# A graph, soft-MoE and MoE model on one core: sort, first linears and first dense stage put in hand-written orders

## The chip, the core and the metric

One core of a Trainium2 chip runs the whole model in one launch. The metric is the device time of a launch in microseconds (us). Five engines work side by side, each through its own queue of instructions: TensorE (PE, whose weight loads the profile lists as PEld), VectorE (DVE), ScalarE (ACT), GpSimd (POOL) and SyncE (SP, which here only issues DMAs). Semaphores order work between engines.

## What is computed

1250 nodes with 768 features, 40,000 edges (src, dst), all in f32. Four residual layers follow one another; the change touches the first two thirds of the first one.

```python
def gatv2(x, src, dst, Ws, bs, Wd, bd, attn):
    H, D = attn.shape
    fs = (x @ Ws + bs).reshape(-1, H, D)
    fd = (x @ Wd + bd).reshape(-1, H, D)
    e = jax.nn.leaky_relu(fs[src] + fd[dst], 0.2)
    logits = jnp.einsum('ehd,hd->eh', e, attn)
    m = jax.ops.segment_max(logits, dst, num_segments=N)
    ex = jnp.exp(logits - m[dst])
    denom = jax.ops.segment_sum(ex, dst, num_segments=N)
    alpha = ex / denom[dst]
    out = jax.ops.segment_sum(alpha[:, :, None] * fs[src], dst, num_segments=N)
    return jax.nn.elu(out)

h = gatv2(x, src, dst, W1s, b1s, W1d, b1d, attn1).reshape(N, DIM)   # 8 heads of 96
h = layer_norm(h + x, ln1_w, ln1_b)
out = gatv2(h, src, dst, Wos, bos, Wod, bod, attno).reshape(N, DIM) # 1 head
return layer_norm(out, lno_w, lno_b)
...
x = x + gnn(layernorm(x));  x = x + soft_moe(layernorm(x))
x = x + gcn(layernorm(x));  x = x + top2_moe(layernorm(x))
```

## The kernel before

Nodes go in 10 blocks of 128 (the last has 98). Softmax over the edges of a node is made dense: for each pair of a block of targets and a block of sources there is a table of logits, 128 x 128 x heads, filled with −3e38 first, into which the edges' logits are scattered. So the kernel has these stages, in order of time of the profiled execution:

- **Sort (0 to 511).** Edges are sorted into the 100 pairs of blocks ("buckets"), 512 places each. `sort_edges` (L202) is a generator. Its first pass makes one-hots of the bucket of each edge on DVE (L250, 63 steps of five columns of 128 edges), which PE adds up (L252); L258 turns the totals into starts. Its second pass goes through the 63 steps again: PE makes running counts (L284, L285), ACT keeps the `carry` to the next step (L287), DVE takes each edge's rank (L290, L292), POOL multiplies the one-hots by node numbers (`valued`, L296), DVE makes for each of five columns a one-hot `to` of the place (L302), and PE permutes with it (L304, two matmuls of 512 columns each, added up in one place in PSUM). At the end the sorted node numbers go to DRAM (`idx_d`) and, by arithmetic on DVE and four transposes, into `where`, the row of each edge in its table.
- **First linears, in the same stretch.** `two_linears` (L789) makes fs and fd per block: transposes of x, then for each of two tables two halves of six matmuls of 384 columns (L801), a copy on ACT (L803), bias and product with `a2` on POOL (L805, L811), a sum per head on DVE (L812), and a store on ACT's queue. After each table the sort goes three steps on. A tile scheduler decides the order on every engine here.
- **Fills.** SP loads edges, x, the weights and biases, then issues 100 fills of 512 KB for the 8-head tables (L1489) and 100 of 64 KB for the 1-head tables (L1493).
- **Branch (511 to 528).** If a bucket overflowed, a general path is taken; otherwise the fast one. All inputs here take the fast one.
- **Edge logits 1 (528 to 1251).** Bucket by bucket, in an order written by hand: rows of fs and fd gathered by one-hot matmuls (L392, f32 split in high and low parts), leaky relu and product on DVE (L404), scattered by POOL (L427). A generator `early` goes one step on per bucket; from bucket 85 on it loads the first dense block's tables.
- **Dense 1 (1286 to 1636).** `Dense.run` (L685). After ACT's queue has issued the loads of fs (L702), ten blocks of targets: maxima over 1250 sources for each of eight heads (`begin`, L717 to L725, DVE); per head ACT's exp over 128 x 1280 (L732), ten PE transposes (L737) whose results DVE multiplies by edge counts ct (`aT`, L738), and the matmuls with fs (L750), one head behind (`waiting`). `end` (L752) divides by the denominators, makes the ELU (an exp on ACT, L768), and calls `normalize` (L836): x + g − 1, statistics by `block_stats` (L144, with a Sqrt on ACT at L151), scale, and weight and bias on POOL. The scheduler decides the order. The logits of a block (`lt`, ten pieces of 512 KB) and counts (`ct`) are loaded on SP's queue (L671 and after), two blocks in the buffers.
- **Linears 2 (to 1810), edges 2 (to 2440), dense 2 (to 2640), soft MoE (to 3200), graph convolution (to 3640), MoE (to 4344).**

`reuse_waits="tile"` pools let a tile wait only for the last users of its own buffer. A DMA signals its end on one of a limited number of semaphores, which later DMAs of other queues use again.

Of the kernel before, what the change touches and what calls it, by code (L numbers as in the profile page):

```python
# [8 lines left out]
F32 = mybir.dt.float32  # L9
# [3 lines left out]
I32 = mybir.dt.int32  # L13
# [37 lines left out]
def model(ctx: ExitStack, tc: tile.TileContext, t: dict, out: bass.AP):  # L51
# [150 lines left out]
    def sort_edges(ap, src_i, dst_i, where, full, bulk):  # L202

        from_b = ap.tile([P, P], BF16, name="from_b")
        nc.vector.tensor_sub(from_b, ones, later)
        minus = ap.tile([1, P], FP16, name="minus")
        nc.vector.memset(minus, -1.0)
        limit = ap.tile([1, 1], F32, name="limit")  # L210
        nc.vector.memset(limit, float(LIMIT))
        ones_b = ap.tile([P, P], BF16, name="ones_b")
        nc.vector.tensor_copy(ones_b, ones)
        bucket = ap.tile([P, NBK], BF16, name="bucket")
        nc.gpsimd.iota(bucket, pattern=[[1, NBK]], base=0, channel_multiplier=0,
                       allow_small_or_imprecise_dtypes=True)
        place = ap.tile([P, CAP], FP16, name="place")
        nc.gpsimd.iota(place, pattern=[[1, CAP]], base=1 - LIMIT, channel_multiplier=0,
                       allow_small_or_imprecise_dtypes=True)


        bk = ap.tile([P, ECOLS], BF16, name="bk")
        in_block = [ap.tile([P, ECOLS], F32, name=f"in_block{i}") for i in range(2)]
        nc.vector.memset(bk, 200.0)
        block = []
        for x, y in zip((src_i, dst_i), in_block):
            nc.vector.memset(y, 0.0)
            hi = ap.tile([P, ECOL + 1], I32, name="hi")
            lo = ap.tile([P, ECOL + 1], I32, name="lo")
            hf = ap.tile([P, ECOL + 1], F32, name="hf", bufs=2)  # L230
            block.append(hf)
            for n, s in ((P, slice(0, ECOL)), (ETAIL, slice(ECOL, ECOL + 1))):
                nc.vector.tensor_scalar(hi[:n, s], x[:n, s], 7, None, op0=ALU.arith_shift_right)
                nc.vector.tensor_scalar(lo[:n, s], x[:n, s], 127, None, op0=ALU.bitwise_and)
                nc.vector.tensor_copy(hf[:n, s], hi[:n, s])
                nc.vector.tensor_copy(y[:n, s], lo[:n, s])
                nc.vector.tensor_scalar_add(y[:n, s], y[:n, s], 1.0)
        for n, s in ((P, slice(0, ECOL)), (ETAIL, slice(ECOL, ECOL + 1))):
            nc.vector.scalar_tensor_tensor(bk[:n, s], block[1][:n, s], float(NB), block[0][:n, s],
                                           op0=ALU.mult, op1=ALU.add)  # L240


        hot = ap.tile([P, 2 * STEPS - 1, LANES, NBK], BF16, name="hot")
        tot_p = bulk.tile([P, 2, 512], F32, name="pair")
        for g in range(STEPS):
            for h in range(2):
                c = (g * 2 + h) * LANES
                if c > ECOL:
                    continue
                nc.vector.tensor_tensor(hot[:, g * 2 + h], bk[:, c:c + LANES, None].to_broadcast([P, LANES, NBK]),  # L250
                                        bucket[:, None, :].to_broadcast([P, LANES, NBK]), ALU.is_equal)
                nc.tensor.matmul(tot_p[:, h, :LANES * NBK], ones_b, hot[:, g * 2 + h].rearrange("p l k -> p (l k)"),  # L252
                                 start=(g == 0), stop=(c + 2 * LANES > ECOL))
        first = ap.tile([1, 2 * LANES + 1, NBK], F32, name="first")
        nc.vector.memset(first[:, 0, :], 0.0)
        for l in range(2 * LANES):
            h, i = divmod(l, LANES)
            nc.vector.tensor_add(first[:, l + 1, :], first[:, l, :], tot_p[0:1, h, i * NBK:(i + 1) * NBK])  # L258
        top = ap.tile([1, 1], F32, name="top")
        over = ap.tile([1, NB, NB], F32, name="over")  # L260
        nc.vector.tensor_scalar_add(over.rearrange("p i j -> p (i j)"), first[:, 2 * LANES, :], float(-CAP))
        nc.vector.tensor_scalar_add(over[:, NB - 1, :], over[:, NB - 1, :], float(P))
        nc.vector.tensor_reduce(top, over.rearrange("p i j -> p (i j)"), AX.X, ALU.max)
        nc.vector.tensor_scalar(full, top, 0.0, None, op0=ALU.is_gt)
        yield

        carry = []
        for h in range(2):  # L270
            x = ap.tile([1, LANES * NBK], FP16, name=f"carry{h}", bufs=2)
            nc.scalar.activation(x, first[:, h * LANES:(h + 1) * LANES, :].rearrange("p l k -> p (l k)"),
                                 AF.Relu, bias=limit, scale=-1.0)
            carry.append(x)
        sorted_p = bulk.tile([P, 2, CAP], F32, name="pair")
        for g in range(STEPS):
            for h in range(2):
                c = (g * 2 + h) * LANES
                if c > ECOL:
                    continue  # L280
                o = hot[:, g * 2 + h]
                flat = o.rearrange("p l k -> p (l k)")
                run = bulk.tile([P, 512], F32, name="run", bufs=2)
                nc.tensor.matmul(run[:, :LANES * NBK], from_b, flat, start=True, stop=False)  # L284
                nc.tensor.matmul(run[:, :LANES * NBK], minus, carry[h], start=False, stop=True)  # L285
                x = ap.tile([1, LANES * NBK], FP16, name=f"carry{h}", bufs=2)
                nc.scalar.activation(x, run[0:1, :LANES * NBK], AF.Relu, scale=-1.0)  # L287
                carry[h] = x
                at = ap.tile([P, LANES, NBK], F32, name="at", bufs=2)
                nc.vector.tensor_tensor(at, run[:, :LANES * NBK].rearrange("p (l k) -> p l k", k=NBK), o, ALU.mult)  # L290
                rank = ap.tile([P, LANES], F32, name="rank", bufs=4)
                nc.vector.tensor_reduce(rank, at, AX.X, ALU.add)  # L292
                valued = []
                for i in range(2):
                    v = ap.tile([P, LANES, NBK], BF16, name=f"valued{i}", bufs=2)
                    nc.gpsimd.tensor_tensor(v, o, in_block[i][:, c:c + LANES, None].to_broadcast([P, LANES, NBK]), ALU.mult)  # L296
                    valued.append(v)
                for l in range(LANES):
                    if c + l > ECOL:
                        continue  # L300
                    to = ap.tile([P, CAP], BF16, name="to", bufs=5)
                    nc.vector.tensor_scalar(to, place, rank[:, l:l + 1], None, op0=ALU.is_equal)  # L302
                    for i in range(2):
                        nc.tensor.matmul(sorted_p[:NBK, i, :], valued[i][:, l, :], to,  # L304
                                         start=(c + l == 0), stop=(c + l == ECOL))
                yield


        nodes = ap.tile([NBK, 2, CAP], F32, name="nodes")
        nodes_b = ap.tile([NBK, 2, CAP], BF16, name="nodes_b")  # L310
        nc.vector.tensor_copy(nodes, sorted_p[:NBK])
        nc.scalar.copy(nodes_b, sorted_p[:NBK])
        nc.sync.dma_start(idx_d[:, :], nodes_b.rearrange("k i c -> k (i c)"))
        row = ap.tile([NBK, CAP], F32, name="row")
        none_at = ap.tile([NBK, CAP], F32, name="none_at")
        nc.gpsimd.iota(none_at, pattern=[[0, CAP // P], [1, P]], base=P * P, channel_multiplier=0,
                       allow_small_or_imprecise_dtypes=True)
        empty = ap.tile([NBK, CAP], F32, name="empty")
        nc.vector.scalar_tensor_tensor(row, nodes[:, 1, :], float(P), nodes[:, 0, :], op0=ALU.mult, op1=ALU.add)
        nc.vector.tensor_scalar_add(row, row, float(-P - 1))  # L320
        nc.vector.tensor_scalar(empty, nodes[:, 0, :], 0.0, None, op0=ALU.is_equal)
        nc.vector.tensor_sub(none_at, none_at, row)
        nc.vector.tensor_mul(none_at, none_at, empty)
        nc.vector.tensor_add(row, row, none_at)
        pt = bank()
        for q in range(CAP // P):
            nc.tensor.transpose(pt[:, q, :NBK], row[:, q * P:(q + 1) * P], ident[:NBK, :NBK])
        nc.vector.tensor_copy(where, pt[:, :, :NBK])
# [1219 lines left out]
```

## Time and profile before

| what | us |
|---|---|
| median of 3 runs (lowest to highest) | 4335.69 (4330.73 to 4339.43) |
| the profiled execution | 4345.71 |
| its span, with a mean granted TensorE clock of 0.923 | 4343.8 |
| busy PE / DVE / ACT / POOL | 3758.5 / 2293.6 / 1156.8 / 1413.5 |
| first one-hot of the count pass (L250) starts | 10.6 |
| last permute (L304) ends | 511.4 |
| first gather matmul (L392) | 527.9 |
| first matmul of the second linears (L801) | 1636.0 |

The span is the profiled program from its first to its last record; times in it are told from its start. Stages overlap little: each needs what the one before wrote to DRAM. The page's second part shows the span in 40 equal slices of 108.6 us, in tenths busy; the first five slices are the sort and first linears, slices 12 to 15 the first dense stage:

```
PE   6888699999958889889999493788969996999998
DVE  8555599999968872277777356430452153000000
ACT  0111166666647661122222111110001121111110
POOL 2444378888851112156666400000001001111111
PEclk7999899999979889999999797898989997999999
DMA  9820122321144441245454531004850015898896
```

### The profile page before, as it was taken

Reading aid. Unit: us, or ns where it says so; the run is one execution under the profiler, and the core shown is the slowest. Engines: PE = TensorE matmul, PEld = TensorE weight load, DVE = VectorE, ACT = ScalarE, POOL = GpSimd, SP = SyncE. Lnnn points to the kernel's source line nnn. Section 1 sums busy time; section 2 is a strip of 40 time slices with the busy share of each in tenths; the row PEclk is TensorE's granted clock in tenths of the full one; section 3 lists DMA queues with packets and bytes.
Section 4 is the critical chain, followed back from the end, with each engine's and each line's share of the span. In section 5 each row is a group of like instructions: output and inputs, shape, how many; then the busy total and the mean of one; then the engine's idle time right before and its main releaser. Section 6 shows DMA issues by size and latency. Waiting matters only on the chain.

```text
span 4343.8 us, 53109 instructions
## 1 busy us (share of the span) xinstructions
PE 3758.5 (87%) x19539; PEld 2911.5 (67%) x19539; DVE 2293.6 (53%) x4014; ACT 1156.8 (27%) x3811; POOL 1413.5 (33%) x1273
## 2 busy tenths in 40 slices
PE   6888699999958889889999493788969996999998
PEld 2444399999958775589999462343436785887876
DVE  8555599999968872277777356430452153000000
ACT  0111166666647661122222111110001121111110
POOL 2444378888851112156666400000001001111111
PEclk7999899999979889999999797898989997999999
DMA  9820122321144441245454531004850015898896
GB/s 319 286 75 19 43 71 56 107 57 53 56 129 164 164 140 41 80 61 59 53 50 50 65 101 61 0 6 107 225 97 30 1 41 191 307 328 325 321 333 225
DMA packets 337404, 531.71 MB, mean 122 GB/s; under 512 B 74136, under 2 KB 211632, under 8 KB 337068
## 3 DMA queue, kind: packets, MB, share of 16 engines
q1 hardware_dynamic: 268848, 461.95, 34.9%
q10 hardware_dynamic: 35772, 43.13, 4.6%
q0 software_dynamic: 32512, 23.13, 2.5%
q8 instruction: 155, 2.54, 0.3%
q14 instruction: 117, 0.96, 0.1%
HBM read 426.11 MB, written 105.82 MB: 122 GB/s over the span
## 4 chain that ended last, share of the span: by engine, by line
PE 51%; DMA 8%; DVE 4%; ACT 4%; issue 3%; POOL 1%; ACTq 0%; SPq 0%; POOLq 0%; DVEq 0%
PE z L392 8%; PE bank L1442 8%; PE acc L1452 7%; PE po L750 5%; PE bank L801 4%; PE acc L185 4%; PE acc L953 3%; ACT ex L732 2%; PE acc L1037 2%; PE acc L978 2%; PE acc L1276 2%; DMA lt<-logit 2%; DMA logit<-lg,where 2%; PE bank L1261 2%; DMA x<-fd_d 1%
## 5 line engine op out<-in xcount | busy, mean ns | idle before, releaser
L427 POOL DMA_INDIRECT logit<-lg,where x780 | 803.3, 1030 | 394.5 <-issue 201.5
L404 DVE SCALAR_TENSOR_TENSOR c<-z,a 128x768 f32<-128x768 f32 x680 | 645.2, 951 | 133.8 <-PE z L392 122.9
L392 PE MATMUL z<-sh,oh 128*128 128x388 f32 (+4 forms) x1560 | 550.5, 353 | 75.5 <-ACT lin L411 38.0
L392 PE MATMUL z<-sl,oh 128*128 128x388 f32 (+4 forms) x1560 | 537.1, 344 | 1.0 <-DVE sl L362 1.0
L392 PE MATMUL z<-dl,oh 128*128 128x388 f32 (+5 forms) x1560 | 536.6, 344 | 0.0
L392 PE MATMUL z<-dh,oh 128*128 128x388 f32 (+5 forms) x1560 | 536.3, 344 | 0.0
L392 PEld LDWEIGHTS z<-sh,oh 128*128 128x128 f32 (+1 forms) x1560 | 301.2, 193 | 85.8 <-ACT lin L411 52.0
L1455 DVE TENSOR_SCALAR y<-acc,sl 128x768 f32<-128x768 f32 x27 | 27.5, 1018 | 591.0 <-PE acc L1452 591.0
L1442 PEld LDWEIGHTS bank<-xT,w 128*128 128x128 f32 x2916 | 330.1, 193 | 10.3 <-issue 8.2
L1442 PE MATMUL bank<-xT,w 128*128 128x128 f32 x2916 | 333.0, 276 | 0.4 <-DVE xT L83 0.4
L750 PE MATMUL po<-fs,aT 128*128 128x97 f32 (+4 forms) x2000 | 320.7, 318 | 3.2 <-POOL fs L697 3.2
L1452 PE MATMUL acc<-w,hT 128*128 128x384 f32 x972 | 321.9, 486 | 0.0
L392 PEld LDWEIGHTS z<-sl,oh 128*128 128x128 f32 (+1 forms) x1560 | 301.1, 193 | 1.7 <-DVE sl L362 1.6
L392 PEld LDWEIGHTS z<-dl,oh 128*128 128x128 f32 (+1 forms) x1560 | 299.8, 192 | 0.0
L392 PEld LDWEIGHTS z<-dh,oh 128*128 128x128 f32 (+1 forms) x1560 | 299.4, 192 | 0.1
L750 PEld LDWEIGHTS po<-fs,aT 128*128 128x128 f32 (+1 forms) x2000 | 259.5, 192 | 56.3 <-issue 7.3
L414 DVE TENSOR_REDUCE lg<-c 128x8 f32<-128x768 f32 x290 | 275.6, 950 | 6.5
L1452 PEld LDWEIGHTS acc<-w,hT 128*128 128x128 f32 x972 | 180.7, 190 | 115.3
L737 PE MATMUL bank<-ident,ex 128*128 128x128 f32 (+1 forms) x900 | 131.7, 301 | 143.3 <-ACT ex L732 139.5
L732 ACT ACTIVATE ex<-lt,top 128x1280 f32<-128x1280 f32 (+1 forms) x90 | 222.5, 2516 | 88.1 <-PE bank L737 65.2
L373 DVE TENSOR_SCALAR oh<-idx,own 128x1024 fp32r<-128x1024 bf16 x200 | 230.2, 1151 | 0.6 <-DMA idx<-idx_d 0.6
L304 PE MATMUL pair<-to,valued 128*100 128x512 bf16 x626 | 169.1, 419 | 69.8 <-DVE to L302 69.6
(318 smaller groups left out, 5769.3 us busy)
## 6 DMA issues: line engine op xcount, KB each, us to landing
w<-in_L_ffn_w_dram SPq DMA_DIRECT2D x53, 3456.0 KB
logit<-none SPq DMA_DIRECT2D x100, 512.0 KB
idx<-idx_d SPq DMA_DIRECT2D x200, 256.0 KB
lt<-logit SPq DMA_DIRECT2D x90, 512.0 KB
w<-in_L_ffn_w_dram SPq DMA_DIRECT2D x32, 576.0 KB
w<-in_L_ffn_w_dram ACTq DMA_DIRECT2D x32, 576.0 KB
logit<-lg,where POOLq DMA_INDIRECT x780, 4.3
ct<-pairs_d SPq DMA_DIRECT2D x18, 576.0 KB
```

The source lines that it names most:

```text
L185: nc.tensor.matmul(p[:n, h, :HF], xT[:, k, b * P:b * P + n], w[:, k, h * HF:(h + 1) * HF], start=(k == 0), stop=(row is None and k == KD - 1))
L304: nc.tensor.matmul(sorted_p[:NBK, i, :], valued[i][:, l, :], to, start=(c + l == 0), stop=(c + l == ECOL))
L373: nc.vector.tensor_scalar(oh, idx.rearrange("p (a c) -> p a c", a=2), own, None, op0=ALU.is_equal)
L392: nc.tensor.matmul(z[:, h, :widths[h]], self.oh[:n, a, q * P:(q + 1) * P], rows[b, w][part][:n, h * HW:h * HW + widths[h]], start=(a == 0 ...
L404: nc.vector.scalar_tensor_tensor(halves(c), self.z[q][:, :, :HF], 0.0, halves(attn), op0=ALU.max, op1=ALU.mult, **more)
L414: nc.vector.tensor_reduce(self.lg[:, q, :], self.c[q].rearrange("p (h d) -> p h d", h=heads), AX.X, ALU.add)
L427: nc.gpsimd.indirect_dma_start(out=table[self.k][:, :], out_offset=bass.IndirectOffsetOnAxis(ap=where[:, q, self.k:self.k + 1], axis=0), i ...
L732: nc.scalar.activation(ex[:n], lt[:n, :, h], AF.Exp, bias=top[:n, h:h + 1])
L750: nc.tensor.matmul(o, aT[:, s, :n], f[:, s, :], start=(s == 0), stop=(s == NB - 1))
L801: nc.tensor.matmul(p[:n, :HF], xT[:, k, :n], w[:, k, h * HF:(h + 1) * HF], start=(k == 0), stop=(k == KD - 1))
L1442: nc.tensor.matmul(pt[:, c - c0, :], w1[:, k, c * P:(c + 1) * P], xT[:, k, :], start=(k == 0), stop=(k == KD - 1))
L1452: nc.tensor.matmul(p[:, h, :HF], hT[:, c, :], w2[:, c, h * HF:(h + 1) * HF], start=(c == 0), stop=(c == KH - 1))
```

## The change

Three stretches are given a fixed order on PE, DVE, ACT and POOL (`manual_schedule`); SP stays with the scheduler.

1. `sort_edges` becomes a class `Sort` whose steps are methods, and the main function writes their order: all one-hots (with the counts five steps behind) together with 12 of the 40 half linears; then `totals` and the rank of step 0; then per step the rank of the next step, 28 half linears spread evenly, and the permute of this step. `to` has 15 buffers instead of 5, `valued` 3 instead of 2, y and c of the linears 3 instead of 2. Loads are issued as src, dst, x0, ws, x1, wd, biases, a2, x2 to x9, and then the fills. Layer statistics are taken block by block, two blocks ahead, instead of for all blocks at the start. In `two_linears` the sum per head and the store come two and three half steps later, and the next block's transposes at the end of the block before.
2. Sorted nodes are copied by ACT into two bf16 tiles and stored; the arithmetic of `where` moves into `rows_in_tables`, called in the fast branch before the first edge logits, with the nodes read back from DRAM by ACT's queue.
3. The first dense stage (heads 8) takes its maxima in a generator of 12 steps and a bit, three of them at each of heads 3 to 7 of the block before; those of block 0 run in the last buckets of the edge stage, two steps per bucket. The end of a block is cut in steps, one per head of the next block. Transposes 8 and 9 of a head come first, and go through an ACT copy and a POOL product instead of DVE. x + g moves to POOL, and its −1 is dropped, since the normalization that follows removes a constant. The order for one head (dense 2) stays.

The core of the diff (the bodies of `one_hot`, `count`, `totals` and the constructor hold the old instructions):

```diff
+        def rank(self, n):
+            _, h, c = self.steps[n]
+            ap, o = self.ap, self.hot[:, n]
+            run = self.bulk.tile([P, 512], F32, name="run", bufs=2)
+            nc.tensor.matmul(run[:, :LANES * NBK], self.from_b, self.flat(n), start=True, stop=False)
+            nc.tensor.matmul(run[:, :LANES * NBK], self.minus, self.carry[h], start=False, stop=True)
+            self.carry[h] = ap.tile([1, LANES * NBK], FP16, name=f"carry{h}", bufs=2)
+            nc.scalar.activation(self.carry[h], run[0:1, :LANES * NBK], AF.Relu, scale=-1.0)
...
+            for i in range(2):
+                v = ap.tile([P, LANES, NBK], BF16, name=f"valued{i}", bufs=3)
...
+                    x = ap.tile([P, CAP], BF16, name="to", bufs=3 * LANES)
+                    nc.vector.tensor_scalar(x, self.place, rank[:, l:l + 1], None, op0=ALU.is_equal)
...
+        def store(self):
+            for i in range(2):
+                nodes = self.ap.tile([P, CAP], BF16, name="to", bufs=3 * LANES)
+                nc.scalar.copy(nodes[:NBK, :], self.sorted_p[:NBK, i, :])
+                nc.sync.dma_start(idx_d[:, i * CAP:(i + 1) * CAP], nodes[:NBK, :])
+
+    def rows_in_tables():
...
+            nc.scalar.dma_start(nodes.rearrange("k i c -> k (i c)"), idx_d[:, :])
...
+            nc.vector.scalar_tensor_tensor(row, nodes[:, 1, :], float(P), nodes[:, 0, :], op0=ALU.mult, op1=ALU.add)
...
+                nc.tensor.transpose(pt[:, q, :NBK], row[:, q * P:(q + 1) * P], ident[:NBK, :NBK])
+            nc.vector.tensor_copy(where, pt[:, :, :NBK])
...
+        def maxima(self, b):
+            n, lt = ROWS[b], self.loaded[b][0]
+            self.tops[b] = top = self.even.tile([P, HEADS], F32, name="top", bufs=2)
+            m = self.even.tile([P, P, self.heads], F32, name="m")
+            nc.vector.tensor_tensor(m[:n], lt[:n, :P, :], lt[:n, P:2 * P, :], ALU.max)
+            yield
+            for j in range(2, NB):
+                nc.vector.tensor_tensor(m[:n], m[:n], lt[:n, j * P:(j + 1) * P, :], ALU.max)
+                yield
+            left = P
+            while left > 32:
+                left //= 2
+                nc.vector.tensor_tensor(m[:n, :left, :], m[:n, :left, :], m[:n, left:2 * left, :], ALU.max)
+                yield
+            nc.vector.tensor_reduce(top[:n], m[:n, :left, :].rearrange("p s h -> p h s"), AX.X, ALU.max)
+            nc.vector.tensor_scalar_mul(top[:n], top[:n], -1.0)
+            yield
+
         def early(self, at):
-            for _ in range(at):
+            for k in range(at):
                 yield
-            yield from self.load(0, self.even)
+            for _ in self.load(0, self.even):
+                k += 1
+                yield
+            if self.heads > 1:
+                while k < NBK - 5:
+                    k += 1
+                    yield
+                for n, _ in enumerate(self.maxima(0)):
+                    if n % 2:
+                        yield
...
+                def end_in_steps(b, po):
...
+                    nc.vector.tensor_scalar_min(neg[:n], g[:n], 0.0)
+                    yield
+                    nc.scalar.activation(neg[:n], neg[:n], AF.Exp)
+                    yield
+                    nc.vector.scalar_tensor_tensor(g[:n], g[:n], 0.0, neg[:n], op0=ALU.max, op1=ALU.add)
+                    yield from finish(dp, b, g)
...
+                        ex = dp.tile([P, NB * P], F32, name="ex", bufs=2)
+                        nc.scalar.activation(ex[:n], lt[:n, :, h], AF.Exp, bias=top[:n, h:h + 1])
+                        aT = dp.tile([P, NB, P], F32, name="aT", bufs=2)
+                        for s0, s1 in ((8, NB), (0, 4), (4, 8)):
+                            pt = pp.tile([P, 4, P], F32, name="bank", bufs=4)
+                            for s in range(s0, s1):
+                                nc.tensor.transpose(pt[:, s - s0, :n], ex[:n, s * P:(s + 1) * P], ident[:n, :n])
+                            if s0 == 8:
+                                raw = dp.tile([P, 2, P], F32, name="raw", bufs=2)
+                                nc.scalar.copy(raw[:, :, :n], pt[:, :2, :n])
+                                nc.gpsimd.tensor_mul(aT[:, s0:s1, :n], raw[:, :, :n], ct[:, s0:s1, :n])
+                            else:
+                                nc.vector.tensor_tensor(aT[:, s0:s1, :n], pt[:, :s1 - s0, :n], ct[:, s0:s1, :n], ALU.mult)
+                        if waiting:
+                            product(*waiting)
+                            if waiting[1] == heads - 1:
+                                ending = end_in_steps(waiting[0], waiting[3])
+                        next(ending, None)
+                        if h >= 3:
+                            for _ in range(3):
+                                next(coming, None)
+                        waiting = (b, h, aT, po)
...
                 x = hb[:n, b, :]
-                nc.vector.scalar_tensor_tensor(x, g[:n], -1.0, x, op0=ALU.add, op1=ALU.add)
+                nc.gpsimd.tensor_add(x, x, g[:n])
+                yield
                 mv = dp.tile([P, 2], F32, name="mv", bufs=2)
+                yield
                 block_stats(mv, x, n)
+                yield
                 nc.vector.tensor_scalar(x, x, mv[:n, 0:1], mv[:n, 1:], op0=ALU.subtract, op1=ALU.mult)
...
+        with tc.manual_schedule(engines={mybir.EngineType.PE, mybir.EngineType.DVE,
+                                         mybir.EngineType.Activation, mybir.EngineType.Pool}):
+            normalize(0)
+            normalize(1)
+            nc.vector.tensor_scalar_mul(a2, a2, 0.2)
+            linears = two_linears(linear_tile, hb, normalize, (ws, wd), biases, a2, HEADS, (fs_d, fd_d))
+            ahead, parts = 5, 12
+            for n in range(steps + ahead):
+                if n < steps:
+                    sort.one_hot(n)
+                if n >= ahead:
+                    sort.count(n - ahead)
+                if n * parts // steps != (n + 1) * parts // steps:
+                    next(linears, None)
+            sort.totals()
+            sort.rank(0)
+            for n in range(steps):
+                if n + 1 < steps:
+                    sort.rank(n + 1)
+                if n * (4 * NB - parts) // steps != (n + 1) * (4 * NB - parts) // steps:
+                    next(linears, None)
+                sort.permute(n)
+            for _ in linears:
+                pass
+            sort.store()
```

In `two_linears`, `run_due()` runs at each half step what has come due:

```diff
+                        behind(2, lambda y=y, c=c, n=n: sum_up(y, c, n))
+                        behind(3, lambda y=y, f_t=f_t, b=b, n=n: store(f_t, y, b, n))
+                        if i == 1 and b + 1 < NB:
+                            turn(b + 1)
```

## The prediction

> **What bounds the kernel now.** I read the stage windows first, then each stage's waits, then the chain. Columns: stretch, length, busy PE, PEld, DVE, ACT, POOL (instructions), granted TensorE clock, DMA share, GB/s.
>
> ```profile
> 0.00:64.00 64.00, 38.58 (x71) 7.51 (x71) 60.97 (x147) 5.93 (x8) 8.19 (x16) 0.70 0.99 349
> 64.00:511.00 447.00, 370.81 (x1284) 194.10 (x1284) 243.44 (x475) 57.24 (x110) 196.96 (x163) 0.92 0.37 122
> 511.00:528.00 17.00, 1.59 (x8) 0.85 (x6) 8.79 (x16) 2.69 (x3) 0.00 (x0) 0.66 0.40 118
> 1286.00:1636.00 350.00, 284.98 (x2406) 278.27 (x2406) 273.71 (x458) 240.77 (x117) 45.95 (x28) 0.88 0.42 150
> ```
>
> The sort's counting is DVE's (60.97 of 64 us) while PE has little to do; linears and permute then take 447 us with no engine full. Two waits there (engine, line, releaser: sum, times, longest) and three lines' durations (min/median/max ns, first to last start) say why:
>
> ```profile
> PE pair L304 <- DVE to L302: 69.6, 60, 3.5
> ACT y L803 <- DMA logit<-none: 16.7, 1, 16.7
> L302 DVE TENSOR_SCALAR to<-place,rank x313: 336/347/1956, 63.4 to 509.0; 128x512 bf16<-128x512 f16 x157
> L1489 SPq DMA_DIRECT2D logit<-none x100: 513/1404/3858, 20.1 to 202.9; - x100
> L1493 SPq DMA_DIRECT2D logit<-none x100: 319/430/1613, 213.5 to 280.9; - x100
> ```
>
> PE waits for `to` at nearly every permute step, and ACT once for a table fill. In the dense stage, the chain (start, us, what) and one row of PE's timeline:
>
> ```profile
> 1382.56 8.03 DMA lt<-logit
> ...
> 1401.63 1.28 ACT L151
> 1402.93 0.20 ACT mv L151
> 1403.15 1.28 ACT L732
> 1404.44 2.70 ACT ex L732
> ...
> 1410.70 1.09 PE bank L737 x10
> 1411.79 2.21 PE po L750 x20
> ```
> ```profile
> 1393.90 2.40 PE L737 MATMUL bank<-ident,ex 128*128 128x128 f32 x10 [6.72 <-ACT ex L732]
> ```
>
> Inside a block PE sets the pace: ten transposes 1.09 and a product 2.21 make 3.30 us a head, 26.4 a block. A block takes 35.9 on average, so 9.5 go at the boundary: waits and ACT's table changes for Sqrt, and transposes at 2.40 instead of 1.09 after PE stood still.
>
> **Part 1: the first stage (0 to 511.4, the last permute).** In the new order the first one-hot stands on DVE behind the scaling of `a2`, whose load stands on SP's queue behind src and dst (0.3 MB), x0, ws, x1, wd and two biases, 7.0 MB in all. At 349 GB/s that is 20 us, with issue and landing about 24; it was 10.6. Pass 1: PE's 12 half linears cost 3.94 each (the chain's "15.75 PE bank L801 x48" is four) = 47, 63 counts of 500 columns 0.21 each = 13, transposes 2; sum 62 us. DVE has 63 one-hots at 0.63 (40). With hand-overs it ends near 92, where the old count ended near 51. Totals and first rank: 6.
>
> Pass 2, PE: 626 permutes at 0.215 (five took 1.24 in a timeline row at 174.69; less a first one of 0.38, a quarter each) = 135, 126 rank matmuls at 0.21 = 26, 28 halves = 110, transposes 5: 276. If nothing else bound, the last permute would come at 92 + 6 + 276 = 374, with its tail 377.
>
> Two things bind more. First, `to`: alone 346 ns, but 904 where a POOL tensor operation runs beside it (87 records). `to` in 15 buffers lets DVE run up to three steps ahead, so I keep of the 69.6 us wait a fifth, 14. Second, ACT's stores of y. In the built program each waits for the transfer that used its completion semaphore before, and these are SP's fills: store 4 for fill 25 of logit1, 5 for 39, up to 8 for 77; 10 for fill 22 of logit2, 11 for 66, 12 for 93, 13 to 19 for 94 to 100. Fills are paced by their bytes: the two rows above give 1.85 us each from 20.1 and 0.68 each from 213.5, so fill 93 has landed at about 277 (the fills may start up to 4 later, as the queue's loads are the same bytes in another order). Behind a waiting store on ACT stand the next `carry` and the copy of y; for `carry` waits PE's next rank, and for that DVE and the permutes. So the lane sets the time: store 12 is issued at half 27 of 40, that is 15 of pass 2's 28 halves, and 46% of pass 2 is left: 128 of PE, plus 14. T = 277 + 128 + 14 = 419, so **−92**. Bounds: 377 if fills do not hold ACT; 445 if all 69.6 stay and fills come late (277 + 128 + 32, and 8). I take 419: the before trace has one such wait, of 16.7 us, on the same pair.
>
> Where this cover is gone: normalizing per block costs DVE about 2 us a block; it runs beside PE's halves and joins the 14 if not.
>
> **Part 2: the branch.** Last permute to first L392 was 16.5 us. Now ACT makes two copies (1.4), SP stores, the branch is decided, and the `where` arithmetic runs inside it: ACT reads idx back, six DVE operations (3.6), four transposes, a copy. First scatters need it; the first L392 needs only SP's loads of fs and fd rows (9 us after the branch), which cover it. **+1**; bounds 0 and +7 (chain uncovered).
>
> **Part 3: edges and change-over.** Block 0's maxima, eight TENSOR_TENSOR at 1.22 to 1.27 (m, L719) and some smaller ones, go into four of DVE's last bucket iterations, each 5.9 us with about 1.3 idle. 12 more less 5 idle: **+7**; bounds 0 and +13. What it should free, the wait before the first exp, is not there to free: the first exp waits for ACT's own queue of fs loads ("27.73 ACTq L702 x16", to 1284.5). **0**.
>
> **Part 4: dense 1 (1286 to 1636).** Maxima leave the block's start and DVE's old boundary chain goes, but a new order is fixed on ACT: exp(h), then the raw copy of transposes 8 and 9, which needs PE to have transposed exp(h), then exp(h+1). One round: hand-over from ACT to PE 0.09, two transposes 0.22, hand-over back 0.19 (gaps in the timeline), copy 0.37 (a 128x256 copy in L85 took 372 ns), exp 2.61 (three in 7.90 at 1404.44, less their gap): 3.48 us, above PE's 3.30. Eight make 27.8. At h=1 ACT waits for neg and runs its exp: 0.84 (L768's mean) and about 1.3 of waiting: 2.1. At h=4 block_stats: ACT stands behind aT, two bn_stats, aggregate and add on DVE, 3.1, then Sqrt 0.2 and two table loads 2.57: 5.8. PE stands still some 6 us there; the row above shows what follows, 2.40 for 1.09. Over two heads that is up to 5.4; I take half, 2.8 (bounds 0 and 5.4). Block: 27.8 + 2.1 + 5.8 + 2.8 = 38.5, where the old was 35.9. POOL's `x+g` (2.4) and its half of `aT` hide under the 3.48 a head. Blocks 2 to 8: 7 × 2.6 = 18. Blocks are measured between their first exps. Block 0 has no ending inside but the low clock of 1251 to 1286: 27.8 + 6 = 34 against 28: +6. Block 1: 38.5 against 40.9: −2. Block 9: 38.5 against 30: +8. **+30**; bounds +10 (no low clock, ACT's waits halved) and +50 (all 5.4, waits doubled).
>
> The Trainium skill speaks against leaving Sqrt between exps: "ScalarE: Activation LUTs", section "Table sets: the hidden batching unit", says to batch by set, and "What ACT_TABLE_LOAD costs" there gives 2.66 us per switch, a drain included. The rows above show 1.28 and the next ACTIVATE 0.02 later. By the page a block would cost 2.75 more, about 25 in all, and the result would be 4307; by the rows it is 4282.
>
> **Sum.** −92 + 1 + 7 + 0 + 30 = −54 (linears 2, edges 2, dense 2 and all later stages keep their instructions). The profiled execution took 4345.7 (span 4343.8 + 1.9), 10 over the median shown; the difference goes against the median: 4335.7 − 54 = 4282, span about 4290 in a like execution. A change under 0.2% (8.7 us, the spread of the three runs) cannot be told from none.
>
> **Rivals.**
> 1. Fills do not hold ACT: T = 377, 42 earlier: 4240. For: in the before trace ACT's stores landed 1.93 us after issue even among fills. Against: the semaphores' order in the built program, and the 16.7 us wait.
> 2. PE keeps its dense pace, ACT's round overlapping: 3.30 × 8 + about 2 = 28.4 a block, 284 against 350: −66 instead of +30: 4186. For: ACT was busy 240.8 of 350 only. Against: exp(h+1) stands behind a copy that needs exp(h) itself.
> 3. The permute still waits for DVE as before: T = 445, 26 later: 4308. For: DVE's pass 2 is 63 × (0.67 + 0.67 + 2.5) + 40 = 282, PE's own size. Against: 15 buffers instead of 5.
> 4. Slower: the maxima of block b+1 stand in DVE's fixed order at head 3, ahead of the next aT. If lt(b+1) has not landed, aT, PE and ACT stand. Before, the chain waited 8.03 for lt at 1382.56, and 9.51 at 1345.32. Nine such blocks, 9 us each: +81, 4363. It decides from (54 + 9)/9 = 7 us a block. Against: SP issues that load at the block's start, it lasts some 16 us (1380 to 1395 at 316 to 410 GB/s), and head 3's first maximum, which needs only two of the ten pieces, comes 13 us in.
>
> **Chances.** Forecast 0.66, rival 1 0.12, rival 2 0.05, rival 3 0.09, rival 4 0.08. Range: the bounds of part 1 reach 4240 and 4308; the dense bounds put 20 to each end of the forecast, part 2 and 3's upper ends 12. 4236 to 4326 holds the forecast's own spread and rivals 1 and 3, and leaves out 2, 4 and the corners, 0.19. Faster: everything but rival 4 and a corner near its upper end, 0.87; within 0.2%: 0.04; slower: 0.09.
>
> **What would show it.** First one-hot near 24; count's end near 92; ACT waiting for fills in 100 to 280, over 100 us in sum; last permute at 419, hardly any wait for `to`; then the first L392 17 us later; dense blocks of 38.5 with exps 3.48 apart, a gap at the fifth head, PE waiting for ACT's exp rather than for DVE. Wrong if ACT shows no wait for fills (then rival 1), if exps are 3.3 apart (2), if DVE is busy throughout 100 to 419 (3), or if L719's successors wait for lt (4).

## The result, and the profile after

The changed kernel takes 4339.27 us (median of 12 runs, 4332.93 to 4352.09), the kernel before 4339.62 in as many runs: a ratio of 1.0002 (95% interval 0.9991 to 1.0014). Nothing moved in the total, where 4282 was forecast. In the stages much moved. The table takes starts of instructions from the traces: the last permute, the first gather matmul of edges 1, the first load of fs, the first exp of dense 1, the first matmul of the second linears, the last gather matmul of edges 2, and the end of the span. The first two traces were taken at different times; the pair marked "again" was run side by side on one chip.

| us | before | after | moved | before, again | after, again | moved |
|---|---|---|---|---|---|---|
| start to last permute | 511.2 | 414.5 | −96.7 | 510.5 | 411.6 | −98.9 |
| to first gather (branch) | 16.7 | 20.9 | +4.2 | 17.0 | 20.7 | +3.7 |
| edges 1 | 726.4 | 741.7 | +15.3 | 726.7 | 737.8 | +11.1 |
| change-over | 31.5 | 32.3 | +0.8 | 32.0 | 31.8 | −0.2 |
| dense 1 | 350.2 | 438.9 | +88.7 | 350.3 | 432.5 | +82.2 |
| linears 2 and edges 2 | 803.2 | 785.3 | −17.9 | 813.1 | 811.7 | −1.4 |
| the rest | 1904.6 | 1902.3 | −2.3 | 1900.0 | 1899.6 | −0.4 |
| span | 4343.8 | 4335.9 | −7.9 | 4349.6 | 4345.7 | −3.9 |

So the sort gained what was forecast, and dense 1 gave it back: +82 to +89 where +30 was forecast.

**The first stage.** The windows of the changed kernel (columns as in the prediction), three waits between 99 and 416, and the fills:

```profile
150.00:200.00 50.00, 46.76 (x181) 24.09 (x181) 42.43 (x78) 8.84 (x17) 31.46 (x28) 1.00 0.86 304
350.00:400.00 50.00, 47.81 (x188) 24.00 (x187) 38.53 (x70) 8.49 (x16) 30.40 (x26) 1.00 0.04 16
```
```profile
ACT y L930 <- PE bank L928: 77.6, 22, 5.6
ACT y L930 <- DVE to L304: 20.6, 6, 3.4
PE pair L313 <- DVE to L304: 16.5, 34, 2.9
```
```profile
L1635 SPq DMA_DIRECT2D logit<-none x100: 319/430/1314, 191.2 to 259.3; - x100
```

PE is busy 94 to 96% of each stretch at a granted clock of 1.00, with the fills running (304 GB/s) and without (16 GB/s), and its wait for `to` fell from 69.6 to 16.5. None of the four engines waits for a fill: in the list of waits of this stretch none names a DMA. The last fill is issued at 259.3, and ACT's store 12 (counted from 0), which was to wait for fill 93 (issued at 256.4), is issued at 292.2. In pass 2 the stores come 19 to 25 us apart until 400. The waiting went the other way: by the profile SP held fills back until stores had landed, 61.0 us in nine waits (in the kernel before 73.9 in ten). The forecast named the right end (419 for 414.5) for the wrong reason: the fills never hold the stage up, and PE's own work sets its length.

**Dense 1.** ACT's timeline over one block, from raw copy of head 7 of the block before to the exp after Sqrt (start, us, what; in brackets the idle time before and what ended it):

```profile
1285.42 0.37 ACT L868 COPY raw<-bank 128x256 f32<-128x256 f32 x1 [0.59 <-PE bank L865]
1290.06 2.60 ACT L860 ACTIVATE ex<-lt,top 128x1280 f32<-128x1280 f32 x1 [4.27 <-DVE top L708]
1293.25 0.37 ACT L868 COPY raw<-bank 128x256 f32<-128x256 f32 x1 [0.58 <-PE bank L865]
1293.52 2.72 ACT L860 ACTIVATE ex<-lt,top 128x1280 f32<-128x1280 f32 x1
1298.18 0.37 ACT L868 COPY raw<-bank 128x256 f32<-128x256 f32 x1 [1.95 <-PE bank L865]
1299.93 0.84 ACT L831 ACTIVATE neg<-neg 128x768 f32<-128x768 f32 x1 [1.38 <-DVE neg L829]
...
1312.71 1.28 ACT L151 ACT_TABLE_LOAD   x1
1317.16 0.20 ACT L151 ACTIVATE mv<-mv 128x1 f32<-128x1 f32 x1 [3.17 <-DVE mv L150]
```

Blocks are 44.5 to 46.1 apart, not 38.5. The round of ACT is as worked out (raw copy 0.58 after the exp, then 0.37). What the forecast has not: 4.27 of waiting for `top`, the maxima that were said to leave the block's start; and 1.95 instead of 0.58 before a raw copy, at the second head after each of three gaps (top, neg, and Sqrt, where it is 1.65 to 3.03), not after one. DVE's timeline over the end of another block shows why `top` is late:

```profile
1444.53 1.22 DVE L697 TENSOR_TENSOR m<-lt 128x1024 f32<-128x1024 f32 x1
1445.78 2.89 DVE L700 TENSOR_TENSOR m<-m,lt 128x1024 f32<-128x1024 f32 x2
1448.60 1.27 DVE L871 TENSOR_TENSOR aT<-bank,ct 128x512 f32<-128x512 f32 x2
1449.79 1.00 DVE L148 BATCH_NORM_STATS2 st<-xk 128x6 f32<-128x384 f32 x2
...
1451.58 3.72 DVE L700 TENSOR_TENSOR m<-m,lt 128x1024 f32<-128x1024 f32 x3
1457.12 1.48 DVE L871 TENSOR_TENSOR aT<-bank,ct 128x512 f32<-128x512 f32 x2 [1.82 <-PE bank L865]
1458.52 0.67 DVE L985 TENSOR_SCALAR xk<-xk,mv 128x768 f32<-128x768 f32 x1
1459.10 6.74 DVE L700 TENSOR_TENSOR m<-m,lt 128x1024 f32<-128x1024 f32 x3
...
1468.81 0.17 DVE L708 TENSOR_SCALAR top<-top 128x8 f32<-128x8 f32 x1
```

At each of heads 3 to 5 DVE has two products (1.3) and three maxima (3.7 or more), 5.0 in all, and at two of them the ending's statistics (1.4) or scale (0.7); at head 6 come the folds and `top` itself (2.0). ACT's round is 3.5. At head 5 the three maxima take 6.74 instead of 3.72, while POOL multiplies by the layer norm's weights (two operations of 2.7 from 1459.27). The sums over dense 1 (line, engine, form, count | busy, mean ns | idle before it):

```profile
L860 ACT ACTIVATE ex<-lt,top 128x1280 f32<-128x1280 f32 (+1 forms) x80 | 212.6, 2658 | 32.9 <-DVE top L708 29.9 <-DMA lt<-logit 2.9
L700 DVE TENSOR_TENSOR m<-m,lt 128x1024 f32<-128x1024 f32 (+1 forms) x72 | 116.1, 1612 | 1.9
```
```profile
1209.00:1648.00 439.00, 327.11 (x2406) 315.47 (x2406) 286.68 (x381) 269.08 (x198) 131.16 (x116) 0.83 0.33 120
```

A maximum takes 1612 ns on average; L719 before took 1280 in its dense stage. PE's granted clock is 0.83, where it was 0.88. And POOL is busy 131 us instead of 46. No engine is full.

### The profile page after: what moved, and what is told of

It is laid out like the page before. It is cut to its first block, busy times and chain, and to the rows that moved or that the text cites. A ratio compares the mean times of both kernels' runs of the same rounds, so it can differ in the third digit from the quotient of the medians.

```text
span 4335.9 us, 53397 instructions
## 1 busy us (share of the span) xinstructions
PE 3750.9 (87%) x19539; PEld 2936.9 (68%) x19539; DVE 2331.7 (54%) x3940; ACT 1186.5 (27%) x3900; POOL 1513.7 (35%) x1363
## 5 line engine op out<-in xcount | busy, mean ns | idle before, releaser
L780 PE MATMUL po<-fs,aT 128*128 128x97 f32 (+4 forms) x2000 | 350.1, 337 | 3.4 <-POOL fs L738 2.3
L1594 DVE TENSOR_SCALAR y<-acc,sl 128x768 f32<-128x768 f32 x27 | 27.5, 1017 | 591.0 <-PE acc L1591 591.0
L1581 PEld LDWEIGHTS bank<-xT,w 128*128 128x128 f32 x2916 | 330.2, 193 | 10.3 <-issue 8.3
L780 PEld LDWEIGHTS po<-fs,aT 128*128 128x128 f32 (+1 forms) x2000 | 289.7, 212 | 57.4 <-issue 7.9
L865 PE MATMUL bank<-ident,ex 128*128 128x128 f32 (+1 forms) x800 | 128.3, 317 | 141.8 <-ACT ex L860 133.2
L432 ACT ACTIVATE c<-c 128x96 f32<-128x96 f32 x800 | 223.9, 301 | 0.0
L860 ACT ACTIVATE ex<-lt,top 128x1280 f32<-128x1280 f32 (+1 forms) x80 | 212.6, 2658 | 32.9 <-DVE top L708 29.9
```

What stands on the lines that cost most here:

```text
L432: nc.scalar.activation(x, x, AF.Copy, accum_out=self.lg[:, q, h:h + 1])
L780: nc.tensor.matmul(o, aT[:, s, :n], f[:, s, :], start=(s == 0), stop=(s == NB - 1))
L860: nc.scalar.activation(ex[:n], lt[:n, :, h], AF.Exp, bias=top[:n, h:h + 1])
L1581: nc.tensor.matmul(pt[:, c - c0, :], w1[:, k, c * P:(c + 1) * P], xT[:, k, :], start=(k == 0), stop=(k == KD - 1))
```

## The experiments

Each group of kernels ran on one chip, with the kernel before beside it; its median there was 4347.5 (group 1, the first four rows), 4390.2 (group 2, the next four), 4354.2 (group 3, the next two) and 4346.4 (group 4, the last two), so totals are compared by ratio and stages by traces. Linears 2 and edges 2 took 785 to 811 us in the first groups' traces, and 848 to 864 in all four of group 2.

| kernel | ratio to before (95%) | last permute | edges 1 | dense 1 |
|---|---|---|---|---|
| sort_only | 0.9799 (0.9783–0.9814) | 412.5 | 725.9 | 345.8 |
| dense_only | 1.0214 (1.0196–1.0232) | 510.7 | 737.2 | 438.8 |
| max_2_per_head | 0.9887 (0.9869–0.9905) | 413.2 | 739.8 | 396.3 |
| no_edge_max | 1.0034 (1.0023–1.0045) | 413.4 | 749.8 | 434.6 |
| max2_stats_early | 0.9865 (0.9839–0.9892) | 413.5 | 740.4 | 369.1 |
| max2_raw_dve | 0.9913 (0.9885–0.9942) | 413.5 | 740.2 | 390.1 |
| max2_both | 0.9859 (0.9833–0.9885) | 412.9 | 736.8 | 362.4 |
| sort_a2_late | 0.9792 (0.9765–0.9819) | 411.0 | 723.7 | 346.9 |
| max0_under_loads | 0.9954 (0.9938–0.9969) | 413.6 | 726.2 | 433.7 |
| max2_neg_later | 0.9798 (0.9782–0.9814) | 412.0 | 737.9 | 349.5 |
| all_together | 0.9772 (0.9738–0.9807) | 410.5 | 724.6 | 346.8 |
| all_sqrt_later | 0.9726 (0.9692–0.9760) | 412.0 | 724.8 | 332.9 |

**1. Each half alone.** `sort_only` is the kernel before with the new sort, linears, loads and `rows_in_tables`; `dense_only` is it with the new `Dense` and `normalize`. Together the two edits are the whole change.

> The new sort and linears with the old dense stage, the old branch order of maxima, and the new place of where. Theory (the two parts add up: the sort's gain was given back in dense 1): last permute near 415 as in the changed kernel, dense 1 back at 350 us, so 4339 - 96 + 4 + 0 to 5 = 4247 to 4257. Rival (the first stage's gain is lost later whatever dense does, because edges or the change-over take longer after it): 4300 or more, with dense 1 at 350.

> The old sort and linears with the new dense stage (maxima of block 0 in the edge stage, normalization in steps). Theory: dense 1 takes about 439 instead of 350 and edges 1 about 10 more, so 4339 + 89 + 10 = 4438. Rival (dense 1 is long only in the company of the new sort): dense 1 near 350 to 380, 4340 to 4380.

Both theories hold: 0.9799 and 1.0214, whose product is 1.0009. Dense 1 is 346 with the old order behind the new sort, and 439 with the new order behind the old sort. The new dense order costs by itself.

**2. Maxima two to a head.**

```diff
-                        if h >= 3:
-                            for _ in range(3):
+                        if h >= 1:
+                            for _ in range(2):
                                 next(coming, None)
```

> The changed kernel with two maxima steps per head from head 1 on, instead of three from head 3 on. Theory (DVE has more work in heads 3 to 6, some 5 us each, than ACT's round of 3.5, so top comes 3 to 4.5 late for the next block): ACT's wait for top goes from 29.9 to under 5, a block from 45 to about 40, the kernel to 4339 - 9 x 4.5 = 4298. Rival 1 (ACT's own round and its waits for neg and Sqrt set the block): no change in blocks beyond the 3.3 of the wait itself being moved, above 4325. Rival 2 (lt of the next block is not there by head 1): DVE waits for lt, blocks stay at 45 or grow, 4340 or more.

Dense 1 fell by 42.6 (4.7 a block, to blocks of 39.8 to 40.8), and ACT's waits are now:

```profile
ACT raw L868 <- PE bank L865: 73.7, 76, 2.9
ACT mv L151 <- DVE mv L150: 31.1, 9, 4.4
...
ACT neg L831 <- DVE neg L829: 11.3, 9, 1.3
ACT ex L860 <- DVE top L708: 2.5, 3, 1.2
```

The wait for `top` went from 29.9 to 2.5, and neither an exp nor a maximum waited for lt: for this part of the loss DVE's order was the cause, neither the transfers (rival 2) nor ACT's round (rival 1).

**3. Block 0's maxima elsewhere.**

```diff
             for _ in self.load(0, self.even):
                 k += 1
                 yield
-            if self.heads > 1:
...
-                for n, _ in enumerate(self.maxima(0)):
```

> The changed kernel with block 0's maxima at the start of the dense stage instead of the last buckets of edges 1. Theory (DVE has under 1 us idle in a late bucket, and the first exp waits for fs loads anyway): edges 1 end some 10 us earlier, and the maxima (13 us) hide under the 31 us of fs loads: 4339 - 10 = 4329. Rival (they were hidden in the edge stage and are not under the loads): 4339 + 13 = 4352.

It did not put them where it was to. One row, the maxima's durations and first and last start:

```profile
L700 DVE TENSOR_TENSOR m<-m,lt x80: 1204/1225/2746, 688.8 to 1602.2; 128x1024 f32<-128x1024 f32 x72, 98x1024 f32<-98x1024 f32 x8
```

They start at 688.8, in the middle of edges 1, as soon as lt was there; edges 1 grew from 741.7 to 749.8. Neither claim was tested, but it shows that the middle of edges 1 covers them no better than its end. `max0_under_loads` gives them a tile from the dense stage's pool, which is free only after edges 1:

```diff
-            m = self.even.tile([P, P, self.heads], F32, name="m")
+            m = (pool or self.even).tile([P, P, self.heads], F32, name="m")
...
+                                for _ in self.maxima(0, dp):
```

> The changed kernel with block 0's maxima on a tile that the edge stage's memory has to free first, so that they can only run after edges 1, beside the loads of fs. The kernel no_edge_max had them only moved to the middle of edges 1 (688 to 772). Theory (in edges 1 PE and DVE are both full and 13 us of maxima cost 13 to 16; under the fs loads they cost nothing): edges 1 at 726 instead of 742, change-over at 32 to 35: 0.4% faster than the changed kernel, ratio to before 0.996. Rival (edges 1 is long for another reason, such as where being made inside the branch): edges 1 stays at 735 or more; ratio 1.000.

Edges 1 is 726.2, as before, and the change-over 33.6. So the 11 to 15 that edges 1 had grown are these maxima, all of them, and beside the fs loads they cost under 2.

**4. The other waits of the fixed order.** On top of two maxima to a head: the statistics on DVE one head before ACT's Sqrt; transposes 8 and 9 on DVE without the raw copy; both; and with both, ACT's exp of the ELU one head later.

```diff
 max2_stats_early, in normalize:
+                st = small.tile([P, 2, 6], F32, name="st")
...
+                nc.vector.bn_aggr(mv[:n, :], st[:n].rearrange("p a s -> p (a s)"))
+                nc.vector.tensor_scalar_add(mv[:n, 1:], mv[:n, 1:], EPS)
                 yield
-                block_stats(mv, x, n)
+                nc.scalar.activation(mv[:n, 1:], mv[:n, 1:], AF.Sqrt)
...
 max2_raw_dve:
-                            if s0 == 8:
...
-                                nc.scalar.copy(raw[:, :, :n], pt[:, :2, :n])
-                                nc.gpsimd.tensor_mul(aT[:, s0:s1, :n], raw[:, :, :n], ct[:, s0:s1, :n])
...
+                            nc.vector.tensor_tensor(aT[:, s0:s1, :n], pt[:, :s1 - s0, :n], ct[:, s0:s1, :n], ALU.mult)
 max2_neg_later, in end_in_steps:
                     yield
+                    yield
                     nc.scalar.activation(neg[:n], neg[:n], AF.Exp)
```

> Two maxima per head from head 1, and the block statistics on DVE one head before ACT's Sqrt. Against 4304 with two maxima per head alone. Theory (at h=4 ACT waits 3.3 to 4.4 for DVE's statistics, and PE comes back at half clock behind that gap): the wait of 31 us in all goes, the table loads of 2.6 stay, the clock comes back partly: 9 x 4 = 36 less, 4268. Rival (the wait only moves to the next raw copy, since DVE's own order is late by as much): 4295 or more, and ACT's wait on PE or DVE grows by what Sqrt no longer waits.

> Two maxima per head from head 1, and transposes 8 and 9 multiplied by DVE again instead of ACT copy and POOL product. Against 4304. Theory (the raw copy ties exp(h+1) to PE's transposes of exp(h); without it ACT runs one exp ahead and its round is 2.65, so PE's 3.30 sets the pace and ACT's waits at neg and Sqrt are covered in part by the exp ahead): 9 x 4 less, about 4265. Rival (DVE is the bound: 31 us of its work per block instead of 28, with POOL beside it): no gain, 4300 or more, top late again by 3 or more.

> Both edits of the two kernels before. Theory: gains add up in part, blocks near 34 to 35, dense 1 near 345 as in the old scheduler order, 4250. Rival (DVE bound): blocks of 37 or more, 4275 or more.

> The kernel max2_both (dense 1 at 362) with ACT's exp of the ELU one head later, and all that follows it. Theory (each of ACT's waits in the fixed order is an idle time that PE pays again at half clock): its 30.5 us of waiting for neg go, dense 1 falls by 15 or more, to 347. Rival (DVE is the bound by now, 31 us of 36): ACT's wait goes over to top, dense 1 stays above 357.

The statistics a head earlier took 27.2 off dense 1 (369.1), less than the 36 expected; Sqrt's wait fell from 31.1 to 0.7, while the wait for `top` grew from 2.5 to 9.1. The raw copy was worth only 6.2 by itself (390.1) and 6.7 on top (362.4): a miss, for 36 were expected, and the ratio of `max2_raw_dve` shows no gain at all (0.9913 against 0.9887). `max2_both` missed too, with 362.4 for 345, and its blocks of 36.5 to 39.1 are the rival's. Without the copy ACT runs ahead and then stands where its inputs are late: for Sqrt 66.9 instead of 31.1, for neg 27.5 instead of 11.3, and at the first exp of each of blocks 1 to 9 for 4.7 to 4.9. The profile puts six of these nine down to lt, but each of these exps starts 0.16 after DVE has finished `top`, so it is `top` that is late again, as the rival had it. The ELU's exp a head later took off 12.9 more (349.5; 15 were expected): nearer the theory than the rival's 357. The wait for neg fell from 29.1 to 6.0, and Sqrt's came back:

```profile
ACT mv L984 <- DVE mv L982: 57.1, 8, 7.2
```

**5. Loads ahead of the first one-hot.** On top of `sort_only`:

```diff
             normalize(0)
-            normalize(1)
-            nc.vector.tensor_scalar_mul(a2, a2, 0.2)
...
+                if n == 8:
+                    normalize(1)
+                if n == 9:
+                    nc.gpsimd.tensor_scalar_mul(a2, a2, 0.2)
```

> The new sort with the old dense stage, and the scaling of a2 on POOL after the tenth one-hot, normalization of block 1 after the ninth. Theory (the first stage is bound by PE from the first one-hot on, and that waits 8.6 us for a2): first one-hot near 12, last permute some 6 to 10 earlier than 413, 4252 scale of the kernel before (0.980) becomes 0.978. Rival (PE's linears wait for ws, wd and the counts for nothing, so the end moves by less than 3): no change.

The first one-hot came at 9.4 instead of 23.1, and the last permute only 1.5 earlier; the ratio cannot be told from sort_only's. DVE then stood 10.3 us for block 1 of x, which lands at 23.9, about when a2 did. So whether the late start costs the stage anything was not settled: one wait took the place of the other.

**6. Same chip, and all together.** The two kernels once more, unchanged, beside each other:

> The kernel before once more, for a trace taken on the same chip as the three runs beside it. Edges 2 has the same instructions in all kernels and took 785 to 811 us in the first five traces and 848 to 864 in the last four. Theory (this differs by chip or execution, not by kernel): edges 2 here and in the changed kernel agree within 12. Rival (the change itself shortens edges 2 by some 18, as the first two traces have it): it is 15 to 20 longer here than in the changed kernel.

> The changed kernel once more, same chip. Stage by stage against the kernel before beside it: last permute 97 earlier, branch 4 longer, edges 1 15 longer, change-over 1, dense 1 89 longer: 12 in sum; the rest by theory within 12, by the rival 18 shorter.

Linears 2 and edges 2 agree within 1.4 there (the first table), so the 17.9 of the first two traces is not put down to the change; the sum of what is, −98.9 + 3.7 + 11.1 − 0.2 + 82.2, is −2. `all_together` is max2_neg_later with the edits of max0_under_loads and sort_a2_late; `all_sqrt_later` puts one more `yield` between the statistics and Sqrt.

```diff
+                yield
                 nc.scalar.activation(mv[:n, 1:], mv[:n, 1:], AF.Sqrt)
```

> max2_neg_later with block 0's maxima beside the fs loads and a2 scaled later on POOL. Theory (the costs add): last permute at 410, edges 1 at 726, dense 1 at 350: 0.9798 - 11/4350 - 2/4350 = 0.977 of the kernel before. Rival (a part is traded: maxima beside the loads delay the first block, or DVE's order in it): dense 1 at 358 or more, ratio 0.980.

> The same with ACT's Sqrt, and the scaling after it, one more head after the statistics. Theory (DVE's order, 31 us of work a block at 35, is the bound, and Sqrt's 57 us of waiting is only where ACT's lead is spent): ACT's wait goes over to top or to the raw transposes, dense 1 within 6 of all_together. Rival (Sqrt's wait is itself on the path, through the exps behind it): dense 1 falls by 15 or more, to 335, ratio 0.974.

The costs add: 0.9772. Then theory fell and the rival all but held: with one more head of distance dense 1 is 332.9, 13.9 less where the theory allowed 6 and the rival asked for 15. So Sqrt's wait was on the path (the edit also moves the scaling and POOL's products behind it by a head; no run separates the two). Dense 1 is now shorter than the old order's 350, and the kernel at 0.9726 (4228.8 against 4346.4) is faster than the kernel before, the changed one and `sort_only`. Its dense 1, what is left of Sqrt's wait, and the end of a block on DVE and ACT:

```profile
1189.50:1522.40 332.90, 287.33 (x2406) 276.47 (x2406) 291.60 (x462) 241.63 (x118) 57.90 (x36) 0.94 0.43 158
```
```profile
ACT mv L979 <- DVE mv L976: 28.0, 8, 3.5
```
```profile
1353.57 0.17 DVE L708 TENSOR_SCALAR top<-top 128x8 f32<-128x8 f32 x1
```
```profile
1353.90 2.65 ACT L855 ACTIVATE ex<-lt,top 128x1280 f32<-128x1280 f32 x1 [4.46 <-PE bank L860]
```

DVE, with the raw copy's work back and 292 of 333 busy, was not the bound at 349. Now it nearly is: in the block from 1320 to 1354 it is busy 31.1 of 33.9, and ACT stands 4.4 in each block until `top` is done. PE's granted clock is 0.94 where the changed kernel's was 0.83.

## Why the prediction was wrong

- **Part 1, the first stage: right size, wrong cause.** −92 forecast, −97 to −99 measured. The first one-hot came at 25.3 (24), the end of the count at 98.9 (92), the last permute at 414.5 (419). The step that failed is PE's own sum: 276 for pass 2 was too little. A step's ten permutes take 2.20 and its two rank matmuls 0.61 from start to start (209.22 to 212.03 in PE's timeline), not 2.15 and 0.42, and a half linear 3.98: 63 × 2.81 + 28 × 3.98 + 5 = 293, and with the 16.5 of waiting for `to` 310, where 308 was measured. At that pace ACT's store 12 comes 36 us after the fill it shares a semaphore with, and rival 1 (fills do not hold ACT) was right on the mechanism, though not on its price. 128 of remaining PE work and a wait at 277 hit the end by chance. That `to` waits nearly vanish (14 forecast, 16.5 measured) was right.
- **Part 2, the branch: +1 forecast, +4.** The step left out, by the trace, is on ACT: the copies of the sorted nodes stand behind the last store of fd, and that waits for DVE's last sum:

```profile
418.86 0.32 ACTq L916 DMA_DIRECT2D fd_d<-y  x1
419.22 1.07 ACT L319 CAST to<-pair 100x512 bf16<-100x512 f32 x2 [5.14 <-DVE y L913]
```

- **Part 3: +7 forecast, +11 to +15** (bounds 0 and +13). The maxima's price was too low: 12 was forecast, and they took 17.6 on DVE, for the two steps of a bucket took 3.98 and 4.06 instead of 2.5 where POOL multiplied beside them. Such a bucket takes 9.2 to 9.3, where the last full ones before took 5.9 to 7.1, and DVE still stands 0.8 in it. That nothing is won at the change-over was right.
- **Part 4, dense 1: +30 forecast, +82 to +89, outside its bounds.** This made the prediction wrong. The failed step is "Maxima leave the block's start", which costed them at nothing and named no cover: 12 steps in four heads give DVE up to 5 us a head against ACT's 3.5, and `top` came 2.9 to 4.5 late in each of blocks 1 to 9; spreading them gave 42.6 back. Second, the low clock was counted after one gap a block, where there are three. The waits for neg (1.3 forecast, 1.4) and Sqrt (3.1, 3.0) were of the right size. In the block from 1245 to 1290, 45.0 against 38.5: `top` 4.3, the raw copies' waits 8.7 where hand-overs of 4.0 and a low clock of 2.8 were allowed, neg 0.2 more; that makes 6.4 of the 6.5.
- **The rivals.** Rival 4 had the right place, DVE's fixed order from head 3 on, its sign and near its price (7 a block to decide; 6.5 more than forecast were lost), with the wrong releaser: it was DVE's own work. The maxima never waited for lt, and the one wait of 2.9 that the profile puts down to it ended, like the other eight, 0.08 after `top` was done. Rival 2 is refuted by the blocks' length, rival 3 by the 16.5 of waiting.
- **The page's rule on table sets.** The Trainium skill ("ScalarE: Activation LUTs", "Table sets: the hidden batching unit") speaks against a Sqrt among exps. Here a load takes 1.28 and the next exp starts 0.02 later, as before, so the price by the rows held; what the order lost at Sqrt was the wait for the statistics (3.0 a block), and the kernel with the Sqrt still among the exps, but farther from its statistics, is the fastest. No run batches the Sqrts, so what that would save is not shown.

## What to carry to other kernels

When an order is written by hand, add up each engine's work per slot of that order (here per head), not per block, and compare it with the round of the engine that sets the pace: 28 us of DVE work fit a block of 35 us and still cost 4.7 us a block, since most of it stood in four heads of eight. Put between the producer and the consumer of a small result (maxima, statistics, an ELU's argument) at least one whole slot, two where the engine that waits runs ahead. And judge a rewrite of several stages stage by stage, with both kernels on one chip: here a gain of 97 to 99 and losses of 82 to 89, 11 to 15 and 4 read as "no change". A wait in a list of waits shows where an engine's lead is spent, not what its end is worth: of Sqrt's 57 us, 29 went away and dense 1 fell by 13.9.

## What was not expected of the hardware

- Linears 2 and edges 2 together, the same instructions but for the order of a few, took 785 to 864 us in sixteen traces, and 848 to 864 in all four of group 2; the two kernels run side by side agreed within 1.4. What sets it was not looked into.
- A DVE maximum of 128 x 1024 took 1.22 us alone, and three took 6.74 while POOL worked on tiles of 128 x 768 beside them. In dense 1 of the changed kernel 26 maxima with no POOL tensor operation beside them took 1.22 each, and 16 with one beside them for over nine tenths of their time 2.71 to 2.74.
- After PE's gap of 6.07 us at Sqrt ten transposes take 2.40 instead of 1.25; after the gaps of 2.2 to 2.7 us at `top` and neg they take 1.3 to 2.1, and the product behind them 3.3 to 4.0 instead of 2.37. In the block from 1245 to 1290 the granted clock is 0.52 from 1250 to 1252.6, 0.62 from 1260.5 to 1263.4 and 0.50 from 1276.4 to 1279, and 1.00 between. The stage's clock was 0.88 before, 0.83 with three such gaps a block, and 0.94 in `all_sqrt_later`, where PE's waits for an exp are 48.9 us (12 times) instead of 133.2 (32 times).
